# Twelve normalized tiles turned by TensorE instead of through DRAM, row units that leave PSUM early, and later transfers in SyncE's order

## The chip, the cores and the metric

The kernel runs on one core of a Trainium2 chip. The core has TensorE (PE) for matrix products, VectorE (DVE), ScalarE (ACT) and GpSimd (POOL) for elementwise work, and SyncE (SP), which here issues nearly all DMA transfers; 16 DMA engines carry them out. Each engine works through its own instructions in order and waits on semaphores for the others. The metric is the device time of one execution in microseconds. Before the change its median is 3538.62 us over 3 runs (3537.95 to 3542.44).

## The reference

One transformer block with conditional normalization, in float32, over x of 8 x 1024 x 512, with 16 heads of width 32 and a hidden width of 2048:

```python
mod = silu(condition) @ Wada + bada
sh_a, sc_a, gt_a, sh_m, sc_m, gt_m = split(mod, 6, axis=1)
xm = layernorm(x, g1, be1) * (1 + sc_a) + sh_a
x = x + gt_a * (softmax(mask(q k^T) * 32 ** -0.5) v @ Wproj + bproj)   # q, k, v = xm @ Wqkv
xm = layernorm(x, g2, be2) * (1 + sc_m) + sh_m
x = x + gt_m * (gelu(xm @ W1 + b1) @ W2 + b2)
```

The mask is causal: a query sees the keys up to its own place.

## The kernel before, in words

**Blocks.** The 8 x 1024 tokens are cut into NB = 16 blocks of 512 tokens, numbered n; an even block is the first half of a sequence, an odd one the second. Every block goes through the first norm (tiles `hat_a`, `xm_a`), the products k, q and v, attention, the output product (`project_out`), the second norm (`hat_m`, `xm_m`), `up` (four steps with a gelu) and `down` (four parts).

**Two streams.** Attention is one stream; the linear work of neighbouring blocks is the other and is woven into it. The linear work follows `plan`: beside block w, roughly the rest of `down` for block w - 2, v, the output product and second norm of block w - 1, k and q for block w + 1, then `up` for w - 1. The order of all instructions is written when the kernel is built. A planner keeps a clock for each engine (`now`), the time at which each result is believed ready (`written`) and the time at which a buffer is free (`left`); `note`, `note_pe`, `note_act` and `note_dma` advance them. `work` advances that thread of linear work which waits least by this reckoning; `step_aside` puts linear work ahead of an attention step whose inputs are not believed ready. `jobs`, `row_jobs` and `act_jobs` are queues of elementwise work, and `sooner` and `either` choose between two engines by the same clocks. On the chip the order is fixed, and an instruction that comes to its place too early holds up everything behind it on its engine.

**Weights.** The linear products use one level of Strassen's scheme on 256 x 256 pieces. The pieces come through a ring of 8 slots (`fetch`, L347 to L363); SyncE issues each load when TensorE has freed the slot. All transfers stand in SyncE's one queue: weights, x, residuals, turned tiles and attention images.

**Turning a normalized tile.** The norm is computed with tokens on partitions, and the products need features there. Tiles named in `by_pe` (a0, a1, m0, m1, m14, m15) are turned by TensorE in `modulated`: for each of four feature chunks four 128 x 128 transposes against the identity go into one of the three PSUM banks (L778), then one VectorE or ScalarE instruction (L782, L788) applies scale and shift on the way to SBUF. All other tiles go through `turn`: VectorE turns 32 x 32 blocks (L714) into the space of `xm`, SyncE writes 1 MB to DRAM as `held` (L723), four transfers of 256 KB bring it back in turned order (L728), and four instructions apply scale and shift. For such tiles x is loaded in another order of rows too (L412 instead of L410).

**Attention by rows.** Odd blocks, and block 0, compute scores twice: once for the row maxima (`scores_at_once`), once transposed for the weights (`weights_T`, exponentials at L1734). Even blocks from 2 on, seven of them, are row blocks (`attend_rows`). A row unit (`rows_unit`) puts the scores of four heads, queries by keys, into `st`, a set of four PSUM banks that is there once for all score work. In the kernel before, VectorE adds the mask in place (L2028), takes the maxima (L2032) and scales them (L2034), and ScalarE reads `st` for the exponentials with their sums and writes `rows_p` in SBUF (L2040). VectorE turns 32 x 32 blocks (`turned`, L2053), SyncE writes an image to DRAM (`scatter`, L2068), and `gather` reads pages of it back in turned order (L2143) for the products with v (L2155). `inverses` sends the reciprocals of the sums the same way (L2097, L2105). There are three SBUF slots for units and pages, and at most two units may stand between scores and image at a time. Each row block has ten units: four of one part with 512 keys, four of two parts with 384 and 128 keys, and two of two parts with 256 keys each. That makes 70 units and 112 parts.

**What sets the order around the change.** The planner's ready times decide where SyncE's transfers stand; a transfer is written into the order when its input is believed ready:

```python
note("DVE", 620, [("hat", key, t)], done)
nc.sync.dma_start(held, small_blocks)
note_dma(2600, [("blocks", key)], [("held", key)])
yield [("held", key)], []
```

Of the kernel before, what the change touches and what calls it, by code (L numbers as in the profile page):

```python
# [9 lines left out]
F32 = mybir.dt.float32  # L10
BF16 = mybir.dt.bfloat16
AF = mybir.ActivationFunctionType
# [10 lines left out]
def kernel(  # L23
# [370 lines left out]
        r0 += n  # L394
    O_G1, O_BE1, O_G2, O_BE2, O_BPROJ, O_B2, O_B1, O_BADA = at

    by_pe = {"a0", "a1", "m0", "m1", f"m{NB - 2}", f"m{NB - 1}"}
    Q = P // NTT

    def hat_tile(key):  # L400
# [305 lines left out]
    def turn(key, rows, xm):  # L706

        small_blocks = xm.rearrange("p c n -> p (c n)")
        by_tile = small_blocks.rearrange("p (m h t i) -> p h m t i", m=NTT, h=NC, t=NTT)
        written["blocks", key] = NEVER  # L710

        def turn_tile(t):
            into = by_tile[:, :, :, t, :]
            nc.vector.transpose(into, rows[:, t, :].rearrange("p (h m i) -> p h m i", m=NTT, i=Q))  # L714
            done = [("blocks", key)] if t == NTT - 1 else []
            note("DVE", 620, [("hat", key, t)], done)

        for t in range(NTT):
            add_job(lambda t=t: turn_tile(t), [("hat", key, t)], key[0] == "m")
        yield [("blocks", key)], []  # L720
        held = kept.tile([P, NTT * D], F32, tag=f"held_{turns[0] % 2}", name=f"held_{key}")
        turns[0] += 1
        nc.sync.dma_start(held, small_blocks)  # L723
        note_dma(2600, [("blocks", key)], [("held", key)])
        yield [("held", key)], []
        for m in range(NTT):
            some = held[:, ts(m, D)].rearrange("(a i) d -> i a d", i=Q)
            nc.sync.dma_start(rows[ts(m, Q), :, :], some)  # L728
            note_dma(1250, [("held", key)], [("turned", key)])
        yield [("turned", key)], []  # L730
# [1267 lines left out]
    def rows_unit(n, g, parts):  # L1998

        until(lambda: n in projected)  # L2000
        until(lambda: free_p and len(raws) < 2)
        slot = take_slot()
        raws.append(slot)
        reads = [("qT", n), ("kT", n)]
        step_aside(reads, ["st", ("p", slot)])
        name = f"{n}_{g}_{parts[0][0]}"
        sc = ps_st.tile([P, HPG, TB], F32, tag="st", name=f"rows_sc_{name}")
        raw = pp.tile([P, HPG * TB], F32, tag=f"p{slot}", name=f"rows_p_{name}")
        mx, minus = (
            small.tile([P, 2, HPG], F32, tag=f"rows_{kind}", name=f"rows_{kind}_{name}")  # L2010
            for kind in ("max", "minus")
        )
        for gg in {part[4]: None for part in parts}:
            if (n, gg) not in totals_of:
                totals_of[n, gg] = small.tile(
                    [P, HPG, NTT], F32, tag=f"rows_sum_{gg}", name=f"rows_sum_{n}_{gg}", bufs=1
                )
        for qt, kh, c0, w, gg in parts:
            for j in range(HPG):
                r = slice(j * hd, (j + 1) * hd)  # L2020
                nc.tensor.matmul(  # L2021
                    sc[:, j, c0 : c0 + w], qTs[n][r, gg, ts(qt, P)], kTs[n][r, gg, :w],
                    start=True, stop=True, skip_group_check=True,
                )
# [3 lines left out]
        nc.vector.tensor_tensor(place, place, shape_of.to_broadcast(place.shape), ALU.add)  # L2028
        note("DVE", 165 + 4.16 * span, ["st"])
        n_parts = len(parts)  # L2030
        for i, (qt, kh, c0, w, gg) in enumerate(parts):
            nc.vector.tensor_reduce(mx[:, i, :], sc[:, :, c0 : c0 + w], axis=AX.X, op=ALU.max)  # L2032
            note("DVE", 170 + 4.14 * w, ["st"], [("mxr", slot)])
        nc.vector.tensor_scalar(minus[:, :n_parts], mx[:, :n_parts], -scale, None, ALU.mult)  # L2034
        note("DVE", 120, [], [("mxr", slot)], port=True)
        places, at = [], 0
        for i, (qt, kh, c0, w, gg) in enumerate(parts):
            tile_of = raw[:, at : at + HPG * w].rearrange("p (b k j x) -> p j k b x", b=NTT, j=HPG, x=hd)
            for j in range(HPG):
                nc.scalar.activation(  # L2040
                    tile_of[:, j], sc[:, j, c0 : c0 + w].rearrange("p (k b x) -> p k b x", b=NTT, x=hd),
                    AF.Exp, bias=minus[:, i, j : j + 1], scale=scale, accum_out=totals_of[n, gg][:, j, qt : qt + 1],
                )
                note_act(480 + 0.82 * w, "exp", ["st", ("mxr", slot)], [("p", slot)])
            places.append((qt, w, gg, at))
            at += HPG * w
            in_sums[n, gg] += 1
            if in_sums[n, gg] == NTT:
                written["sums", n, gg] = written["p", slot]
                start(inverses(n, gg))  # L2050

        def turned():
            nc.vector.transpose(raw, raw)  # L2053
            note("DVE", 2320, [("p", slot)], [("p", slot)])
            start(scatter())

        def scatter():
            yield [("p", slot)], []
            for qt, w, gg, at in places:
                count = w // P  # L2060
                if (n, gg) not in images:
                    images[n, gg] = [
                        kept.tile([P, 2, NTT, size, P], F32, tag=f"image_{gg}_{size}", name=f"image_{n}_{gg}_{size}")
                        for size in (2, 4)
                    ]
                for a in range(NTT):
                    into = images[n, gg][qt // 2][:, qt % 2, a, :count, :]
                    nc.sync.dma_start(  # L2068
                        into.rearrange("(b k) s e -> k b (s e)", k=hd),
                        raw[ts(a, hd), at : at + HPG * w].rearrange("k (b f) -> k b f", b=NTT),  # L2070
                    )
# [12 lines left out]
    def inverses(n, g):  # L2084

# [202 lines left out]
```

## Time and profile before

| what | us |
|---|---|
| median of 3 runs | 3538.62 |
| the profiled execution | 3545.22 |
| its span, first to last instruction | 3543.5 |
| TensorE busy | 3377.7 |
| VectorE busy | 2339.5 |
| GpSimd busy | 1762.9 |
| ScalarE busy | 1248.8 |

Busy time is the time in which an engine worked on instructions. Matmuls overlap in TensorE, so one that is shown with 379 ns follows the one before it much sooner, and a group of four on different columns of the array runs at the same time. The mean granted clock of TensorE over the execution is 0.985 of its full rate. A row of the waits names who waited, for whom, the total, the number and the longest. A row of the groups gives line, engine, operation, tiles, shapes and count, then busy time and mean ns of one, then the engine's idle time before them and what ended it. The chain of work is followed back from the last instruction, at each step to what released it.

### The profile page before, as it was taken

To read this page: it belongs to the slowest core of one execution; us is meant where nothing else is said; L and a number is where in the kernel's file an instruction comes from. 1 tells how busy PE (TensorE), PEld (TensorE's weight loads), DVE (VectorE), ACT (ScalarE), POOL (GpSimd) and SP (SyncE) were. 2 spreads that over 40 slices of the span, in tenths; PEclk is the share of its full clock that TensorE was granted. 3 is DMA by queue.
4 is the path that set the end of the run, shared out by engine and by line. 5 is a ranking of instruction groups with operands and counts; after the bars stand their busy time and mean duration, and the time that the engine had idled before them with its cause. 6 is when DMAs were issued, how large, how long until landed. Compare 5 with 4: busy or idle time off the path is not lost.

```text
span 3543.5 us, 118795 instructions
## 1 busy us (share of the span) xinstructions
PE 3377.7 (95%) x52861; PEld 1705.4 (48%) x52861; DVE 2339.5 (66%) x2562; ACT 1248.8 (35%) x1970; POOL 1762.9 (50%) x1710
## 2 busy tenths in 40 slices
PE   8999889999899998999999999999999999899999
PEld 4444445444454444544454454544555445454455
DVE  5766577657577575775767757676677667566563
ACT  2334333343233532335223353333523334232521
POOL 3667713756037650477405674066731667208640
PEclk9999999999999999999999999999999999999999
DMA  6843487537875378753886538865498555973344
GB/s 198 263 148 112 150 235 214 155 109 213 245 209 155 102 226 239 209 153 103 247 233 189 153 109 264 253 185 142 127 284 236 147 142 154 284 221 111 92 135 138
DMA packets 502579, 645.42 MB, mean 182 GB/s; under 512 B 40365, under 2 KB 334061, under 8 KB 498485
## 3 DMA queue, kind: packets, MB, share of 16 engines
q1 hardware_dynamic: 501952, 637.80, 60.8%
q8 instruction: 416, 6.82, 0.8%
q14 instruction: 95, 0.77, 0.1%
q10 hardware_dynamic: 116, 0.03, 0.0%
HBM read 506.31 MB, written 129.27 MB: 179 GB/s over the span
## 4 chain that ended last, share of the span: by engine, by line
PE 37%; DMA 6%; POOL 4%; DVE 3%; issue 1%; SPq 1%; ACT 1%; DVEq 0%; POOLq 0%; ACTq 0%
PE bank L217 27%; PE sc L1613 3%; POOL pT L1856 3%; PE po L1762 2%; PE st L1721 2%; DMA held_m<-xm_m 1%; DMA turned<-image 1%; PE rows_sc L2021 1%; PE st L1709 1%; PE po L2155 1%; DVE mx L1628 1%; DMA w<-in_L_cond_Wproj_dram 1%; DMA hat_m<-held_m 1%; PE bank L1783 0%; DMA w<-in_L_cond_W_dram 0%
## 5 line engine op out<-in xcount | busy, mean ns | idle before, releaser
L1856 POOL TENSOR_TENSOR pT<-pT,pT 128x512 f32<-128x512 f32 (+3 forms) x918 | 981.9, 1104 | 250.5 <-ACT pT L1734 197.2
L217 PE MATMUL bank<-w,hT 128*32 128x256 f32 x14336 | 822.4, 380 | 0.9 <-ACT y_d L204 0.9
L1734 ACT ACTIVATE pT<-st 128x2048 f32<-128x2048 f32 x218 | 409.5, 1879 | 762.1 <-PE st L1721 573.9
L217 PEld LDWEIGHTS bank<-w,hT 128*32 128x32 f32 x14336 | 457.0, 110 | 372.7 <-issue 87.5
L1628 DVE TENSOR_REDUCE mx<-sc 128x4 f32<-128x2048 f32 (+3 forms) x271 | 499.4, 1859 | 183.0 <-PE sc L1613 179.7
L217 PE MATMUL bank<-xm_m,w 128*32 128x256 f32 x8192 | 506.6, 384 | 28.8 <-DMA w<-in_L_cond_W_dram 19.7
L2040 ACT ACTIVATE rows_p<-rows_sc,rows_minus 128x256 f32<-128x256 f32 (+3 forms) x448 | 229.6, 534 | 448.0 <-DVE rows_minus L2034 246.4
L217 PE MATMUL bank<-t_m,w 128*32 128x256 f32 x6144 | 382.9, 380 | 1.1 <-DVE hT L208 0.9
L217 PEld LDWEIGHTS bank<-xm_m,w 128*32 128x32 f32 x8192 | 257.8, 111 | 245.5 <-issue 66.4
L217 PEld LDWEIGHTS bank<-t_m,w 128*32 128x32 f32 x6144 | 190.7, 110 | 179.8 <-issue 58.3
L217 PE MATMUL bank<-xm_a,w 128*32 128x256 f32 x3968 | 252.1, 392 | 26.0 <-DVE xm_a L782 16.3
L217 PE MATMUL bank<-w,qT 128*32 128x512 f32 x2048 | 242.0, 610 | 16.3 <-DMA w<-in_L_cond_Wproj_dram 16.2
L1613 PE MATMUL sc<-kT,qT 32*128 32x512 f32 (+3 forms) x2168 | 250.6, 546 | 6.9 <-DVE mx L1628 3.5
L1762 PE MATMUL po<-pT,v 128*32 128x512 f32 (+3 forms) x2176 | 232.0, 515 | 4.5 <-POOL pT L1739 4.4
L1721 PE MATMUL st<-qT,kT 32*128 32x512 f32 (+3 forms) x2176 | 228.5, 508 | 0.0
L208 DVE TENSOR_TENSOR hT<-bank,u_u 128x512 f32<-128x512 f32 x181 | 121.4, 683 | 113.0 <-PE bank L217 110.6
L217 PEld LDWEIGHTS bank<-xm_a,w 128*32 128x32 f32 x3968 | 131.7, 113 | 131.3 <-issue 29.2
L217 PE MATMUL bank<-t_a,w 128*32 128x256 f32 x2944 | 184.4, 383 | 2.6 <-DVE qT L208 2.1
L2053 DVE STREAM_TRANSPOSE rows_p<-rows_p 128x2048 f32<-128x2048 f32 x70 | 160.9, 2298 | 36.2 <-ACT rows_p L2040 35.5
L1625 DVE TENSOR_TENSOR sc<-sc,mask 128x1024 f32<-128x1024 f32 (+1 forms) x89 | 90.5, 1017 | 124.4 <-PE sc L1613 91.9
L1129 ACT ACTIVATE hT<-hT,cols 128x512 f32<-128x512 f32 x256 | 164.4, 711 | 22.8 <-DVE hT L208 21.6
L655 POOL TENSOR_SCALAR rstd_a<-mv_a 128x4 f32<-128x4 f32 x14 | 3.2, 231 | 333.6 <-DVE mv_a L634 333.1
(268 smaller groups left out, 4152.9 us busy)
## 6 DMA issues: line engine op xcount, KB each, us to landing
w<-in_L_cond_W_dram SPq DMA_DIRECT2D x384, 256.0 KB
w<-kept_up_S SPq DMA_DIRECT2D x256, 256.0 KB
w<-kept_down_S SPq DMA_DIRECT2D x256, 256.0 KB
w<-kept_qkv_S SPq DMA_DIRECT2D x180, 256.0 KB
w<-in_L_cond_Wqkv_dram SPq DMA_DIRECT2D x147, 256.0 KB
image<-rows_p SPq DMA_DIRECT2D x112, 256.0 KB
turned<-image SPq DMA_DIRECT2D x28, 1024.0 KB
turned<-image SPq DMA_DIRECT2D x56, 512.0 KB
```

The source lines that it names most:

```text
L208: nc.vector.tensor_tensor(out, src, other, op)
L217: nc.tensor.matmul(ps[r, :], columns, rhs, start=start, stop=stop, skip_group_check=True)
L1129: nc.scalar.activation(hT[:, i, :], hT[:, i, :], AF.Gelu, bias=cols[:, O_B1 + f : O_B1 + f + 1])
L1613: nc.tensor.matmul(sc[:, j, c0 : c0 + w], qTs[n][r, gg, ts(qt, P)], keys_of(n, kh)[r, gg, :w], start=True, stop=True, skip_group_check=True,)
L1625: nc.vector.tensor_tensor(place, place, shape_of.to_broadcast(place.shape), ALU.add)
L1628: nc.vector.tensor_reduce(maxima[n, gg][:, kh, qt, :], sc[:, :, c0 : c0 + w], axis=AX.X, op=ALU.max)
L1721: nc.tensor.matmul(st[:, j, c0 : c0 + w], kT[r, gg, ts(k % NTT, P)], qT[r, gg, TB - w :], start=False, stop=True, skip_group_check=True,)
L1734: nc.scalar.activation(pT[:, :, :used], st[:, :, :used], AF.Exp, scale=scale)
L1762: nc.tensor.matmul(po[r, TB - w :], v[:, k % NTT, g * P + j * hd : g * P + (j + 1) * hd], pT[:, j, c0 : c0 + w], start=(k == 0), stop=last ...
L1856: nc.gpsimd.tensor_tensor(into, into, pT[:, j, c0 : c0 + w], ALU.add)
L2040: nc.scalar.activation(tile_of[:, j], sc[:, j, c0 : c0 + w].rearrange("p (k b x) -> p k b x", b=NTT, x=hd), AF.Exp, bias=minus[:, i, j : j ...
L2053: nc.vector.transpose(raw, raw)
```

## The change

Four things change.

1. `by_pe` gets a5, a7, ... a15 and m3, m5, ... m13. These twelve tiles are the ones that are turned while an even block is attended by rows.
2. `rows_unit` empties `st` at once: VectorE adds the mask to the last 128 keys of each part while it writes them to `rows_p`, and ScalarE copies the other keys, 128 at a time. The maxima are a job of its own (`largest`), the exponentials a thread of its own (`exponentials`), and both work on `rows_p` in SBUF, in place. The small tiles for maxima get two buffers by name.
3. Four ready times are set later: blocks of a turned tile by 1200 ns, `held` by 2500, a turned row unit by 2000, the rows of reciprocals by 2500.
4. Nothing else is edited, but as the order is planned, instructions move on all engines. Counted in the order: TensorE has 192 more transposes, VectorE 48 fewer of its block transposes, SyncE 60 fewer transfers, ScalarE 168 more copies; the table loads of ScalarE are 6 more, and some elementwise work changes its engine.

```diff
-    by_pe = {"a0", "a1", "m0", "m1", f"m{NB - 2}", f"m{NB - 1}"}
+    by_pe = (({"a0", "a1", "m0", "m1", f"m{NB - 2}", f"m{NB - 1}"}) | {f"a{n}" for n in range(5, NB, 2)}) | {f"m{n}" for n in range(3, NB - 1, 2)}
...
             note("DVE", 620, [("hat", key, t)], done)
+            for one in done:
+                written[one] += 1200
...
         note_dma(2600, [("blocks", key)], [("held", key)])
+        written["held", key] += 2500
...
-        span, place = diagonals(parts, sc)
-        shape_of = mask.unsqueeze(1).unsqueeze(1)
-        nc.vector.tensor_tensor(place, place, shape_of.to_broadcast(place.shape), ALU.add)
-        note("DVE", 165 + 4.16 * span, ["st"])
-        n_parts = len(parts)
-        for i, (qt, kh, c0, w, gg) in enumerate(parts):
-            nc.vector.tensor_reduce(mx[:, i, :], sc[:, :, c0 : c0 + w], axis=AX.X, op=ALU.max)
-            note("DVE", 170 + 4.14 * w, ["st"], [("mxr", slot)])
-        nc.vector.tensor_scalar(minus[:, :n_parts], mx[:, :n_parts], -scale, None, ALU.mult)
         places, at = [], 0
-        for i, (qt, kh, c0, w, gg) in enumerate(parts):
+        shape_of = mask.rearrange("p (b x) -> p b x", x=hd).unsqueeze(1)
+        for qt, kh, c0, w, gg in parts:
             tile_of = raw[:, at : at + HPG * w].rearrange("p (b k j x) -> p j k b x", b=NTT, j=HPG, x=hd)
-            for j in range(HPG):
-                nc.scalar.activation(
-                    tile_of[:, j], sc[:, j, c0 : c0 + w].rearrange("p (k b x) -> p k b x", b=NTT, x=hd),
-                    AF.Exp, bias=minus[:, i, j : j + 1], scale=scale, accum_out=totals_of[n, gg][:, j, qt : qt + 1],
+            into = tile_of[:, :, w // P - 1]
+            some = sc[:, :, c0 + w - P : c0 + w].rearrange("p j (b x) -> p j b x", x=hd)
+            nc.vector.tensor_tensor(into, some, shape_of.to_broadcast(into.shape), ALU.add)
+            for k in range(w // P - 1):
+                nc.scalar.copy(
+                    tile_of[:, :, k],
+                    sc[:, :, c0 + k * P : c0 + (k + 1) * P].rearrange("p j (b x) -> p j b x", x=hd),
                 )
...
+        def largest():
+            for i, (qt, w, gg, at) in enumerate(places):
+                some = raw[:, at : at + HPG * w].rearrange("p (a j x) -> p j a x", j=HPG, x=hd)
+                nc.vector.tensor_reduce(mx[:, i, :], some, axis=AX.XY, op=ALU.max)
+            ...
+            start(exponentials())
+
+        def exponentials():
+            yield [("mxr", slot)], []
+            for i, (qt, w, gg, at) in enumerate(places):
+                some = raw[:, at : at + HPG * w].rearrange("p (a j x) -> p j a x", j=HPG, x=hd)
+                for j in range(HPG):
+                    nc.scalar.activation(
+                        some[:, j], some[:, j], AF.Exp, bias=minus[:, i, j : j + 1], scale=scale,
+                        accum_out=totals_of[n, gg][:, j, qt : qt + 1],
+                    )
+            ...
+            row_jobs.append((turned, [("p", slot)]))
 
         def turned():
             nc.vector.transpose(raw, raw)
             note("DVE", 2320, [("p", slot)], [("p", slot)])
+            written["p", slot] += 2000
             start(scatter())
...
-        row_jobs.append((turned, [("p", slot)]))
+        row_jobs.append((largest, [("raw", slot)]))
...
         note_dma(150, ["rec"], [("rows back", n, g)])
+        written["rows back", n, g] += 2500
```

More of the change, by code (lines that the diff above doesn't have):

```diff
@@ L2009, in rows_unit @@
         mx, minus = (
-            small.tile([P, 2, HPG], F32, tag=f"rows_{kind}", name=f"rows_{kind}_{name}")
+            small.tile([P, 2, HPG], F32, tag=f"rows_{kind}", name=f"rows_{kind}_{name}", bufs=2)
             for kind in ("max", "minus")
@@ L2043, in rows_unit @@
                 )
-                note_act(480 + 0.82 * w, "exp", ["st", ("mxr", slot)], [("p", slot)])
+                note_act(585, None, ["st"], [("raw", slot)])
             places.append((qt, w, gg, at))
             at += HPG * w
[L2047 to L2050, printed above, removed]
+        def largest():
+            for i, (qt, w, gg, at) in enumerate(places):
+                some = raw[:, at : at + HPG * w].rearrange("p (a j x) -> p j a x", j=HPG, x=hd)
+                nc.vector.tensor_reduce(mx[:, i, :], some, axis=AX.XY, op=ALU.max)
+                note("DVE", 170 + 4.14 * w, [("raw", slot)], [("mxr", slot)])
+            n_parts = len(places)
+            nc.vector.tensor_scalar(minus[:, :n_parts], mx[:, :n_parts], -scale, None, ALU.mult)
+            note("DVE", 120, [], [("mxr", slot)], port=True)
+            start(exponentials())
@@ new lines, in exponentials @@
+        def exponentials():
[7 more added lines that the diff above has]
+                    )
+                    note_act(480 + 0.82 * w, "exp", [("mxr", slot)], [("p", slot)])
+                in_sums[n, gg] += 1
+                if in_sums[n, gg] == NTT:
+                    written["sums", n, gg] = written["p", slot]
+                    start(inverses(n, gg))
+            row_jobs.append((turned, [("p", slot)]))
```

2 lines of the change are left out of this document (1 added, 1 removed).

## The prediction

> **What bounds the kernel now.** I read the page's head first, then a table of stages, then TensorE's waits, then the chain of work through one of those waits.
>
> ```profile
> span 3543.5 us, 118795 instructions
> PE 3377.7 (95%) x52861; PEld 1705.4 (48%) x52861; DVE 2339.5 (66%) x2562; ACT 1248.8 (35%) x1970; POOL 1762.9 (50%) x1710
> ```
>
> TensorE is busy for 3377.7 of 3543.5 us. No other engine passes 66%, so the end is TensorE's own work plus the 165.8 us in which it stands. The table of stages says where it stands. Each row gives a stretch, then the busy time of TensorE, its weight loads, VectorE, ScalarE and GpSimd, the granted clock, the DMA share and GB/s. The first row is a stretch without row blocks; the other seven are the early parts of the row blocks 2, 4, 6, ... 14.
>
> ```profile
> 200.00:300.00 100.00, 100.00 (x1496) 47.54 (x1496) 63.38 (x72) 49.21 (x49) 65.16 (x69) 1.00 0.44 126
> 400.00:500.00 100.00, 78.41 (x1039) 36.09 (x1032) 65.23 (x75) 34.00 (x101) 33.78 (x35) 0.88 0.66 198
> 850.00:950.00 100.00, 84.37 (x1312) 44.33 (x1304) 62.04 (x83) 24.04 (x71) 24.26 (x21) 0.95 0.92 272
> 1300.00:1400.00 100.00, 84.46 (x1300) 42.93 (x1300) 58.21 (x78) 22.16 (x62) 13.06 (x13) 0.93 0.86 258
> 1750.00:1850.00 100.00, 90.91 (x1412) 48.55 (x1416) 57.87 (x75) 22.28 (x48) 11.62 (x11) 0.93 0.85 246
> 2150.00:2250.00 100.00, 89.58 (x1456) 49.22 (x1452) 60.62 (x82) 21.43 (x61) 22.20 (x20) 0.97 0.92 281
> 2600.00:2700.00 100.00, 89.51 (x1416) 47.25 (x1412) 60.52 (x78) 24.10 (x60) 10.30 (x10) 0.95 0.89 258
> 3025.00:3125.00 100.00, 87.84 (x1396) 46.87 (x1392) 56.53 (x75) 23.52 (x59) 15.19 (x14) 0.97 0.84 247
> ```
>
> The seven stretches idle for 100 minus their second figure: 21.6, 15.6, 15.5, 9.1, 10.4, 10.5 and 12.2, together 94.9 us. In the six later ones the DMA engines are 84% to 92% busy and the granted clock is 0.93 to 0.97; in the first row the DMA is at 44%, the clock at 1.00 and TensorE never idle. What TensorE waits for (total, times, longest):
>
> ```profile
> PE bank L217 <- DMA w<-in_L_cond_W_dram: 19.7, 3, 7.5
> PE po L2155 <- DMA turned<-image: 17.1, 19, 3.2
> PE bank L217 <- DVE xm_a L782: 16.3, 2, 8.6
> PE bank L217 <- DMA w<-in_L_cond_Wproj_dram: 16.2, 11, 4.5
> PE rows_sc L2021 <- ACT rows_p L2040: 12.5, 4, 7.9
> PE bank L217 <- ACT xm_m L788: 2.8, 2, 2.1
> PE sc L1613 <- ACT rows_p L2040: 2.1, 2, 1.4
> ```
>
> These seven rows are 86.7 us. The chain at block 8 (start, length, what), and the turn of block 5 in order of time, show what stands behind them:
>
> ```profile
> 1784.94 10.20 DMA held_m<-xm_m
> ...
> 1796.50 7.43 DMA hat_m<-held_m
> ...
> 1804.47 5.01 DMA w<-in_L_cond_W_dram
> ```
>
> ```profile
> 876.27 0.33 SPq L723 DMA_DIRECT2D held_a<-xm_a  x1
> ...
> 897.04 1.01 DVE L782 TENSOR_SCALAR xm_a<-hat_a,gaina,shifta 128x512 f32<-128x512 f32 x2 [4.11 <-DMA hat_a<-held_a]
> ...
> 897.64 0.65 PE L217 MATMUL bank<-xm_a,w 128*32 128x256 f32 x4 [8.65 <-DVE xm_a L782]
> ```
>
> A turn through DRAM takes 876.27 to 897.04, 20.8 us from write to use, and in block 8 1784.94 to 1803.93, 19.0 us. The weight of the next step comes after it in SyncE's queue (issued 1804.47) and TensorE stands again.
>
> **The change, part by part.**
>
> *The turn.* Twelve tiles (a5 to a15 and m3 to m13, odd) leave the DRAM route. What goes and what one costs:
>
> ```profile
> held_m<-xm_m SPq DMA_DIRECT2D x12, 1024.0 KB
> hat_m<-held_m SPq DMA_DIRECT2D x48, 256.0 KB
> L714 DVE STREAM_TRANSPOSE xm_m<-hat_m 128x512 f32<-128x512 f32 x48 | 30.2, 679 | 0.0
> L728 SPq DMA_DIRECT2D hat_m<-held_m x48: 303/424/1413, 687.4 to 3085.0; - x48
> ```
>
> Per tile one write and four reads go, 2 MB, and five issues at about 0.42 us. At 272 GB/s (stretch 850 to 950) 2.1 MB are 7.7 us of all DMA engines, so two tiles free about 15 us of some 92 busy in each of six stages. VectorE loses 48 transposes of 0.679, 32.6 us, with none idle before them. The loads of x keep their count and bytes. Added are 192 transposes on TensorE, four to a bank:
>
> ```profile
> 211.39 0.66 PE L778 MATMUL bank<-ident,hat_m 128*128 128x128 f32 x4
> 211.97 0.42 PE L217 MATMUL bank<-t_a,w 128*32 128x256 f32 x4
> L778 PE MATMUL bank<-ident,hat_m x64: 272/273/477, 211.4 to 3440.6; 128*128 128x128 f32 x64
> ```
>
> From a group's start to the next matmul are 0.58 us, change of form included; 48 groups make 27.8 us. The bounds are 0 (all in time in which TensorE stands anyway) and 192 x 0.272 = 52 us (nothing overlaps). I take 27.8: it is the cost in a stretch without idle time. TensorE may also wait for a bank to be emptied, as these rows show for the tiles that it turns already:
>
> ```profile
> PE bank L778 <- DVE xm_m L782: 1.3, 1, 1.3
> PE bank L778 <- ACT xm_a L788: 1.2, 1, 1.2
> ```
>
> That is 0 for m0 and about 1.2 for m1 and a1: bounds 0 and 14 for twelve tiles; I take half of the upper per tile, 6 (nearest to the mean of the tiles shown). Scale and shift remain four per tile, now from a bank on ScalarE or VectorE; these have room (24% and 62% in the stretch 850 to 950).
>
> Against that the two waits for xm_a (16.3) and those for xm_m (2.8) go, since write, landing, read and landing go. The weight waits: W stands behind the turn in the queue, so I take 15 of 19.7 (bounds 19.7 and 0). Wproj comes ahead of the block's own m turn and is helped only by the lower DMA load: 5 of 16.2 (same bounds). Pages of turned rows compete with the same traffic: 8 of 17.1 (bounds 17.1 gained and 17.1 lost, as the margins below hold pages longer).
>
> *The row units.* Today the bank set "st" of a unit is released after mask, maxima and exponentials. Afterwards mask and copies release it, and maxima and exponentials work in SBUF.
>
> ```profile
> L2028 DVE TENSOR_TENSOR rows_sc<-rows_sc,mask 128x1024 f32<-128x1024 f32 x42 | 51.3, 1221 | 27.6 <-PE rows_sc L2021 27.3
> L2028 DVE TENSOR_TENSOR rows_sc<-rows_sc,mask 128x512 f32<-128x512 f32 x28 | 19.3, 691 | 10.6 <-PE rows_sc L2021 10.5
> L2032 DVE TENSOR_REDUCE rows_max<-rows_sc 128x4 f32<-128x2048 f32 x28 | 64.2, 2292 | 1.0
> L2040 ACT ACTIVATE rows_p<-rows_sc,rows_minus 128x512 f32<-128x512 f32 x112 | 75.5, 686 | 163.6 <-DVE rows_minus L2034 48.2 <-DMA turned<-image 34.6 <-issue 27.5
> L197 ACT COPY hT<-bank 128x512 f32<-128x512 f32 x41 | 23.9, 582 | 96.4 <-PE bank L217 96.3
> ```
>
> For the widest unit the release falls from 0.69 + 2.29 + 4 x 0.69 = 5.7 us to three copies of 0.58 beside a mask of 0.69, 1.7 us. ScalarE gets 168 copies x 0.582 = 98 us, 14 per row block; the masks become 112 x 0.691 = 77.4 instead of 70.6. Both lie beside TensorE while ScalarE is under 25% busy there; without that cover the 14 us per block delay every later unit. Maxima and exponentials keep count and size; from SBUF I cost them at nothing (bounds a tenth either way, 23 us over the run, off the path). The waits of rows_sc and sc for rows_p are 14.6: I take 12 (bounds 14.6 gained; 14 lost, one block's copies).
>
> *The margins.* The planner now believes that blocks are ready 1.2 us later, held and rows back 2.5 and turned units 2.0, so it writes these transfers and their readers later. SyncE stands with everything behind it when one comes too early:
>
> ```profile
> SPq L360 <- PE bank L217: 949.2, 478, 20.1
> SPq L723 <- DVE xm_a L714: 31.4, 6, 16.5
> SPq L2068 <- DVE rows_p L2053: 29.9, 13, 7.1
> SPq L723 <- DVE xm_m L714: 16.2, 3, 7.0
> SPq L728 <- DMA held_m<-xm_m: 14.8, 9, 3.4
> ```
>
> The last four are 92.3 us, against 949.2 in which the queue waits for TensorE to free weight slots. Behind them stand the weights. I gave their worth to the weight and page waits above. The price is that a slot of a unit is held some 2 us longer and pages start later; the work of the other steps hides it while there is some, else it is the page bound above.
>
> *The clock.* The stretches with gaps have 0.93 to 0.97. If all 527 us busy in the six ran at 1.00 instead of a mean of 0.95, 26 us would go; I take 6, as most of the low share lies in the gaps themselves (bounds 15 and 0).
>
> *Sum.* 27.8 + 6 - 16.3 - 2.8 - 15 - 5 - 8 - 12 - 6 = -31.3 us. The profiled execution took 3545.2 (span 3543.5 and 1.7 around it), so 3513.9. It lies 6.6 over the median of 3538.6, which gives **3507**.
>
> **A rule that speaks against it.** In the full stretch 200 to 300 TensorE turns tile m0 between other work, and the granted clock stays at 1.00. If the clock fell to half while TensorE turns a tile, the 27.8 would double and the sum be -3.5, 3535; the 0.88 to 0.97 of the other stretches shows that it does fall when TensorE does too little. The Trainium skill, "TensorE: Matmul & The Clock Gate", Part 4, says that transposes do not count as activity for the clock gate in the way matmuls do; by that rule this case would come, and the row of 200 to 300 does not agree with it.
>
> **The rivals.**
> - *Queue order, not volume, is the limit* (slower). The weight waits remain since SyncE's queue is held by free slots (949.2), not by turns, and pages come later and double their 17.1: 27.8 + 6 - 19.1 - 12 + 17.1 = +19.8, **3558**. It decides when W, Wproj and pages together give back less than 3 us. For it: that figure. Against: W is issued 0.5 us after the turn's landing.
> - *ScalarE holds "st"* (slower). Copies stand behind the previous unit's exponentials, 8 x 0.69 = 5.5 us; if this hits 10 of 70 units and the 12 gained go: -31.3 + 12 + 55 = +36, 3574. Against: 24% busy.
> - *All of it goes*: 86.7 of waits and 15 of clock against 33.8: -68, **3471**.
> - *The waits only move*: weight and page waits stay as they are, clock too: 33.8 - 31.1 = +3, 3541.
> - *The clock falls in the turns*: 3535, as worked out above.
>
> **How the numbers follow.** Forecast 0.50, all goes 0.18, queue order 0.15, ScalarE 0.06, waits move 0.06, clock 0.05. Within 0.2% (7 us, about what a measurement of this kernel tells from no change) are the last two, 0.11; faster 0.68, slower 0.21. The range runs from 3471 to the queue case, 3558; only the ScalarE case and the tails of its neighbours lie outside. The forecast's own range is 3485 to 3528.
>
> **What would show it.** Transposes: 288 instead of 96, a group near 0.6 us to the next matmul. Idle in the six later stretches down from 73 to about 35 us, no wait of TensorE on xm_a, W waits under 5. rows_sc waits on ScalarE under 3. DMA 25 MB less in all. If page waits rise above 17 us or W stays near 20, the queue case holds; if rows_sc waits on copies, the ScalarE case.

## The result, and the profile after

The changed kernel takes 3581.47 us (median of 4 runs, 3575.97 to 3588.03), the kernel before 3539.32 us (4 runs, 3537.95 to 3542.44) beside it. The ratio is 1.0119, with a 95% interval from 1.0099 to 1.0138: slower by 1.2%. The forecast was 3507, the range ended at 3558.

The head of the profile after:

```profile
span 3582.2 us, 119193 instructions
PE 3396.4 (95%) x53053; PEld 1715.4 (48%) x53053; DVE 2344.8 (65%) x2575; ACT 1367.2 (38%) x2161; POOL 1725.9 (48%) x1671
```

The span grew by 38.7 us: TensorE is busy 18.7 us longer, with 192 more transposes in it, and stands 185.8 us instead of 165.8. The stretches that the prediction looked at, taken anew for the changed kernel (columns as before). The six later ones begin 31 to 35 us after the first row unit of their block; in the kernel before they began 32 to 68 us after it:

```profile
200.00:300.00 100.00, 99.24 (x1436) 45.49 (x1432) 66.08 (x74) 42.05 (x40) 66.83 (x67) 1.00 0.43 125
420.00:520.00 100.00, 87.11 (x1244) 41.35 (x1240) 80.81 (x93) 51.01 (x142) 15.44 (x18) 0.95 0.82 236
850.00:950.00 100.00, 94.84 (x1500) 51.23 (x1492) 63.33 (x80) 34.87 (x102) 21.20 (x19) 0.98 0.79 240
1280.00:1380.00 100.00, 94.22 (x1532) 50.02 (x1528) 58.83 (x74) 27.36 (x72) 25.60 (x22) 1.00 0.82 249
1710.00:1810.00 100.00, 94.53 (x1476) 52.14 (x1480) 62.56 (x75) 27.07 (x70) 30.39 (x24) 0.95 0.80 238
2145.00:2245.00 100.00, 90.02 (x1396) 47.36 (x1388) 63.31 (x76) 31.45 (x87) 35.70 (x26) 0.97 0.81 242
2585.00:2685.00 100.00, 93.00 (x1496) 50.75 (x1492) 65.63 (x80) 31.46 (x87) 35.67 (x26) 1.00 0.86 262
3025.00:3125.00 100.00, 92.44 (x1456) 49.37 (x1445) 64.77 (x78) 31.46 (x87) 35.69 (x26) 0.98 0.82 255
```

The six later stretches stand 5.2 + 5.8 + 5.5 + 10.0 + 7.0 + 7.6 = 41 us instead of 73; 35 were forecast. With the offsets of before they stand 44 us. In the place looked at, the forecast nearly came true. The loss is elsewhere. A table of stages that counts whole stages, the seven row blocks first (from the first row unit to the first transposed scores of the next block), then, from 73 us on, all that lies between them, gives these sums of length and of TensorE's busy time. The kernel before:

```profile
sum 1447.20, PE 1336.41; mean PE 190.92
sum 2022.80, PE 1981.11; mean PE 247.64
```

The kernel after:

```profile
sum 1352.90, PE 1247.70; mean PE 178.24
sum 2156.40, PE 2090.45; mean PE 261.31
```

The row stages became 94 us shorter and the others 134 us longer. Idle time is 110.8 and 41.7 us before, 105.2 and 66.0 after: what went in the early part of the row stages came back in their later part and in the stages between. TensorE's waits after:

```profile
PE po L2177 <- DMA turned<-image: 31.6, 21, 4.5
PE st L1712 <- DVE mx L1631: 16.3, 13, 3.9
PE sc L1616 <- DVE mx L1631: 14.9, 12, 2.4
PE bank L1786 <- ACT hT L204: 13.4, 3, 4.5
PE bank L217 <- ACT p_k L197: 10.4, 5, 2.4
...
PE sc L1616 <- ACT rows_p L2038: 6.3, 7, 1.0
PE sc L1616 <- DVE rows_p L2035: 6.1, 7, 0.9
PE bank L217 <- DVE u_v L208: 5.6, 3, 2.3
PE bank L217 <- DMA w<-in_L_cond_Wproj_dram: 5.4, 1, 5.4
PE bank L1669 <- DVE mcols L1653: 5.3, 5, 1.4
...
PE rows_sc L2024 <- DVE rows_p L2035: 4.6, 1, 4.6
PE bank L1669 <- POOL mcols L1653: 4.0, 3, 1.6
```

W (the waits for `in_L_cond_W_dram`) is gone from this list, of `xm_a` 0.2 us is left, and Wproj fell from 16.2 to 5.4. In their place stand waits for VectorE and ScalarE. The group of the new copies on the page, and one place in order of time, show how such a wait comes about:

```profile
L2038 ACT COPY rows_p<-rows_sc 128x512 f32<-128x512 f32 x168 | 89.9, 589 | 370.5 <-DVE rows_p L2035 287.7
```

```profile
2554.14 5.35 DVE L167 TENSOR_TENSOR xr<-xr,row_gbm 128x512 f32<-128x512 f32 x4
...
2559.41 3.42 DVE L1229 TENSOR_TENSOR hT<-hT 128x1024 f32<-128x1024 f32 x2
...
2562.76 0.68 DVE L2035 TENSOR_TENSOR rows_p<-rows_sc,mask 128x512 f32<-128x512 f32 x1
2563.53 0.59 ACT L2038 COPY rows_p<-rows_sc 128x512 f32<-128x512 f32 x1 [11.66 <-DVE rows_p L2035]
...
2565.35 0.59 ACT L204 COPY hT<-bank 128x512 f32<-128x512 f32 x1
...
2566.09 1.52 PE L1786 MATMUL bank<-pT,ones 128*32 128x512 f32 x8 [4.48 <-ACT hT L204]
```

A copy (L2038) does not run beside the mask (L2035) of its unit: it starts 0.77 us after the start of the mask, which takes 0.68, since it waits on a semaphore for the mask. Both read `rows_sc`, in the same four banks of `st`, and both write `rows_p`; which of the two the semaphore guards is taken up in the last section. The mask stands behind 8.8 us of other work on VectorE, so ScalarE stands for 11.66 us with a copy at its head; behind that copy is the one that empties a bank (L204), and TensorE stands for the bank. The planner doesn't know: it books the copy with `["st"]` as all it waits for.

### The profile page after: what moved, and what is told of

Same layout as the page of the kernel before. It is cut to its first block, busy times and chain, and to the rows that moved or that the text cites. A ratio compares the mean times of both kernels' runs of the same rounds, so it can differ in the third digit from the quotient of the medians.

```text
span 3582.2 us, 119193 instructions
## 1 busy us (share of the span) xinstructions
PE 3396.4 (95%) x53053; PEld 1715.4 (48%) x53053; DVE 2344.8 (65%) x2575; ACT 1367.2 (38%) x2161; POOL 1725.9 (48%) x1671
## 4 chain that ended last, share of the span: by engine, by line
PE 68%; DVE 13%; DMA 8%; POOL 4%; ACT 3%; issue 2%; SPq 2%; ACTq 0%; DVEq 0%; POOLq 0%
PE bank L217 47%; PE sc L1616 5%; PE po L1765 5%; PE st L1724 5%; DMA turned<-image 4%; DVE mx L1631 3%; POOL pT L1859 2%; PE st L1712 2%; PE po L2177 1%; DMA image<-rows_p 1%; DVE rows_max L2049 1%; ACT rows_p L2038 1%; PE rows_sc L2024 1%; PE bank L1786 1%; DVE rows_p L2035 1%
## 5 line engine op out<-in xcount | busy, mean ns | idle before, releaser
L1859 POOL TENSOR_TENSOR pT<-pT,pT 128x512 f32<-128x512 f32 (+3 forms) x918 | 996.1, 1119 | 304.5 <-ACT pT L1737 135.6
L217 PE MATMUL bank<-w,hT 128*32 128x256 f32 x14336 | 823.1, 382 | 9.1 <-DVE y_d L208 5.1
L217 PEld LDWEIGHTS bank<-w,hT 128*32 128x32 f32 x14336 | 455.7, 110 | 379.2 <-issue 86.2
L217 PE MATMUL bank<-xm_m,w 128*32 128x256 f32 x8192 | 504.7, 381 | 4.7 <-DVE p_u L194 2.4
L217 PE MATMUL bank<-t_m,w 128*32 128x256 f32 x6144 | 381.4, 380 | 3.3 <-DVE hT L208 1.5
L217 PEld LDWEIGHTS bank<-xm_m,w 128*32 128x32 f32 x8192 | 252.4, 110 | 236.4 <-issue 62.7
L217 PEld LDWEIGHTS bank<-t_m,w 128*32 128x32 f32 x6144 | 191.8, 110 | 169.2 <-issue 40.2
L2061 ACT ACTIVATE rows_p<-rows_p,rows_minus 128x256 f32<-128x256 f32 (+3 forms) x448 | 245.3, 551 | 60.0 <-DVE rows_minus L2052 59.8
L217 PE MATMUL bank<-xm_a,w 128*32 128x256 f32 x3968 | 245.1, 383 | 10.4 <-ACT p_k L197 10.4
L217 PE MATMUL bank<-w,qT 128*32 128x512 f32 x2048 | 241.9, 613 | 8.3 <-DMA w<-in_L_cond_Wproj_dram 5.4
L2038 ACT COPY rows_p<-rows_sc 128x512 f32<-128x512 f32 x168 | 89.9, 589 | 370.5 <-DVE rows_p L2035 287.7
L1650 POOL CAST mcols<-mx 128x16 bf16<-128x16 f32 x31 | 13.0, 419 | 418.4 <-DVE mx L1645 402.1
L217 PE MATMUL bank<-t_a,w 128*32 128x256 f32 x2944 | 184.5, 381 | 0.8 <-DVE qT L208 0.8
L217 PEld LDWEIGHTS bank<-xm_a,w 128*32 128x32 f32 x3968 | 128.9, 111 | 116.6 <-issue 29.2
```

The costliest lines, as they stand in the source:

```text
L217: nc.tensor.matmul(ps[r, :], columns, rhs, start=start, stop=stop, skip_group_check=True)
L1859: nc.gpsimd.tensor_tensor(into, into, pT[:, j, c0 : c0 + w], ALU.add)
L2038: nc.scalar.copy(tile_of[:, :, k], sc[:, :, c0 + k * P : c0 + (k + 1) * P].rearrange("p j (b x) -> p j b x", x=hd),)
L2061: nc.scalar.activation(some[:, j], some[:, j], AF.Exp, bias=minus[:, i, j : j + 1], scale=scale, accum_out=totals_of[n, gg][:, j, qt : qt ...
```

## The experiments

Theories put up first. A: the row units cost, because ScalarE's copies stand behind VectorE's mask. B: a turn on TensorE isn't worth its 21 us of work, the stalls only move. C: the order before is fitted to its constants, and any other order costs. Formed on the way, and tested in the later runs: A2, it isn't the copies' wait that costs but that the planner is not told of it; D, deferring maxima and exponentials makes pages late; E, the row stages hold too little linear work. All times are in us; idle is the span less TensorE's busy time in the profiled execution.

| run | edit against the kernel before | median | ratio to before, 95% | idle |
|---|---|---|---|---|
| e1 | turn | 3562.52 | 1.0046 [1.0024, 1.0068] | 158.5 |
| e2 | units | 3588.56 | 1.0126 [1.0103, 1.0149] | 197.8 |
| e3 | later times ("margins") | 3559.77 | 1.0047 [1.0030, 1.0063] | 184.8 |
| e4 | turn, margins | 3571.41 | 1.0075 [1.0049, 1.0101] | 171.5 |
| e7 | turn, m tiles only | 3556.88 | 1.0026 [1.0010, 1.0041] | 180.2 |
| e8 | turn, a tiles only | 3558.12 | 1.0037 [1.0016, 1.0058] | 151.2 |
| e9 | units, copies ahead of the mask | 3586.02 | 1.0108 [1.0091, 1.0125] | 212.3 |
| e11 | nothing but a constant, 110 ns | 3559.88 | 1.0040 [1.0026, 1.0054] | 184.3 |
| e14_sync_90 | the same constant, 90 ns | 3568.61 | 1.0068 [1.0050, 1.0086] | 194.3 |
| e14_sync_120 | the same, 120 ns | 3567.87 | 1.0067 [1.0052, 1.0082] | 191.0 |
| e12 | units, nothing deferred | 3667.21 | 1.0339 [1.0321, 1.0358] | 273.8 |
| e10 | units, booking put right ("told") | 3550.12 | 1.0016 [1.0006, 1.0027] | 170.3 |
| e23 | units, constant 110 | 3621.33 | 1.0216 [1.0196, 1.0237] | 235.8 |
| e24 | units told, constant 110 | 3575.14 | 1.0075 [1.0048, 1.0101] | 192.7 |
| e16 | the whole change, told | 3548.23 | 1.0007 [0.9996, 1.0019] | 148.8 |
| e17 | turn, units told | 3543.81 | 0.9991 [0.9976, 1.0006] | 139.5 |
| e21 | turn of a tiles, units told | 3541.80 | 0.9989 [0.9975, 1.0003] | 156.5 |
| e25 | as e17, pages expected later | 3532.39 | 0.9970 [0.9956, 0.9984] | 134.4 |

### The parts, one at a time

e1, the turn alone:

```diff
-    by_pe = {"a0", "a1", "m0", "m1", f"m{NB - 2}", f"m{NB - 1}"}
+    by_pe = (({"a0", ...}) | {f"a{n}" for n in range(5, NB, 2)}) | {f"m{n}" for n in range(3, NB - 1, 2)}
```

> The kernel before with the longer by_pe alone: TensorE turns the twelve tiles, row units and ready times as before. Theory A (the row units are what costs: ScalarE's copies stand behind VectorE's mask and hold up ScalarE's queue): turning alone gains, since the waits for xm_a (16.3 us) and W (19.7 us) go for about 21 to 28 us of transposes; 3515 to 3530. Theory B (the turn is not worth its work: TensorE pays 21 us and the stalls only move): 3550 to 3560. Theory C (any change of the order costs, since the order before is fitted to the constants): 3550 to 3570 here, and the same in the other two single edits.

e2, the row units alone (the diff of `rows_unit`, nothing else):

> The kernel before with the new row units alone, no further turns, ready times as before. Theory A: block 2 gains up to 20 us, as its waits on st go, but the later blocks lose 8 to 12 us each; 3555 to 3590. Theory B: 3515 to 3530, as only the gain of block 2 is left. Theory C: 3550 to 3570.

e3, the four later times alone, and e4, turn and later times:

```diff
+                written[one] += 1200
+        written["held", key] += 2500
+            written["p", slot] += 2000
+        written["rows back", n, g] += 2500
```

> The kernel before with the four later ready times alone. Theory A: 3530 to 3545, little either way. Theory B: the same. Theory C: 3550 to 3570. If the margins are what makes pages late, the waits of the products with v for pages (17.1 us before, 31.6 after the change) rise here to about 30 us.

> The change without its row units: longer by_pe and later ready times. Theory A: faster than before, 3505 to 3525, the wait of the sum of weights for a bank that ScalarE empties (13.4 us after the change) is gone. Theory B: 3550 to 3560. Theory C: 3560 to 3580.

Each part alone is slower, and the units by most, 1.26% where the whole change is 1.19%. So the first half of theory A, by which e1 and e4 would be faster, does not hold. In e3 the page waits are 25.8 us (about 30 were expected if the later times make pages late), W is 0.6 and Wproj 37.4. TensorE's waits in the run of the turn:

```profile
PE rows_sc L2021 <- ACT rows_p L2040: 27.5, 11, 7.9
PE bank L778 <- DVE y_d L208: 22.6, 6, 5.0
...
PE po L2155 <- DMA turned<-image: 12.7, 11, 2.8
```

W and `xm_a` are gone here too. But the third group of transposes waits for a bank whose content (`y_d`) VectorE is to take out, and VectorE first works through a row unit's mask and maxima:

```profile
828.74 2.29 DVE L2032 TENSOR_REDUCE rows_max<-rows_sc 128x4 f32<-128x2048 f32 x1
...
832.53 0.68 DVE L208 TENSOR_TENSOR y_d<-bank,p_d 128x512 f32<-128x512 f32 x1
...
833.27 1.12 PE L778 MATMUL bank<-ident,hat_a 128*128 128x128 f32 x4 [4.33 <-DVE y_d L208]
```

The wait of the row units for `st` is 27.5 here, 12.5 before. With the units the maxima stand elsewhere: in the changed kernel the `y_d` wait ahead of transposes is 2.2 us.

e7 and e8 split the turn:

```diff
+    by_pe = {... as before ...} | {f"m{n}" for n in range(3, NB - 1, 2)}     # e7
+    by_pe = {... as before ...} | {f"a{n}" for n in range(5, NB, 2)}         # e8
```

> The kernel before with only m3 to m13 turned by TensorE. If the price of turning is the bank that an a tile must wait for (22.6 us of TensorE's waits on y_d, all at hat_a in the run with all turns), these waits are absent here and W stays gone: 10 us of transposes against 19.7 of W, so 3530 to 3540. If turning never pays since the stalls only move: 3550 or more.

> The kernel before with only a5 to a15 turned by TensorE. If the bank is the price: about 20 us of waits on y_d against 16.3 of xm_a, and 10 us of transposes, W stays at 15 to 20: 3555 to 3570. If it is not: no wait on y_d above 5 us.

The halves cost 0.26% and 0.37%, together somewhat more than the whole turn. The ranges of single times are wide (3545.7 to 3574.4 and 3541.8 to 3574.5) and the two profiled executions lie at opposite ends, so their idle times say little. The wait on `y_d` is 16.6 us in e8 and absent in e7, as expected; but e7 is slower than the kernel before as well, where 3530 to 3540 was expected, so that bank is not the whole price of turning. W is 1.5 in e8, though the m tiles still go through DRAM there, and 0.6 in e3, where all twelve tiles do. That W stands because of the turn is therefore not shown.

### What an order is worth

e11 and its two fellows change no work, only the planner's constant for a semaphore. Some instructions change places, and a few elementwise ones their engine (in e11 VectorE has 2559 instead of 2562, ScalarE 1973 instead of 1970, GpSimd 1706 instead of 1710):

```diff
-    SYNC, PIPE, SWITCH, TABLE = 100, 250, 150, 1283
+    SYNC, PIPE, SWITCH, TABLE = 110, 250, 150, 1283
```

> The kernel before with the planner's constant for one semaphore at 110 instead of 100 ns: no instruction is added or removed, only the order moves. If the order before is fitted to its constants (theory C), 3550 to 3565. If not, within 7 us of the kernel before.

> The kernel before with the planner's constant for a semaphore 90 ns instead of 100: no instruction is added or removed, some stand elsewhere. Theory C (the order before is fitted; every other order costs): slower by 0.2 to 0.6%, 3552 to 3567, with the added idle time in a few single waits, in the stretch up to 425 us too. If the effect of order is without direction: between 3525 and 3565, and faster as likely as slower.

> The same with 120 ns. Theory C: slower by 0.2 to 0.8%, 3552 to 3575. Without direction: 3525 to 3565.

All three are slower, by 0.40 to 0.68%. With 110 ns most of the added idle time lies ahead of the first row unit. The sums for the stretch from 73 to 425 us, before and with 110 ns:

```profile
sum 352.00, PE 338.16; mean PE 338.16
```

```profile
sum 352.00, PE 324.54; mean PE 324.54
```

That is 13.8 us of idle time against 27.5, 13.7 of the 18.5 us that e11 stands longer. With 90 and 120 ns it is only 7.4 of 28.5 and 4.8 of 25.2. With the later times of e3 the stretch stands 20.8, in the changed kernel 20.1 from 72.9 to 418.4. So the 0.46 and 0.47% of e1 and e3 are no more than a mere change of order costs: three orders of three speak for theory C. That the order before was fitted is argued, not shown, and not every other order costs: e16, e17 and e25 below, with other work in them, are no slower than the kernel before.

### What makes the units cost

e9 lets the copies go first:

```diff
+            for k in range(w // P - 1):
+                nc.scalar.copy(...)
             nc.vector.tensor_tensor(into, some, shape_of.to_broadcast(into.shape), ALU.add)
-            for k in range(w // P - 1):
-                nc.scalar.copy(...)
```

> The new row units alone, with ScalarE's copies written ahead of VectorE's mask in each part, so that ScalarE need not wait for VectorE (287.7 us of ScalarE's waits after the change). If ScalarE's queue behind the mask is what costs: that wait is gone, and the time falls from 3589 to 3555 or lower. If the longer way of a unit (pages late, work shifted) costs: it stays within 10 us of 3589.

The time stays. The wait has changed sides:

```profile
DVE rows_p L2038 <- ACT rows_p L2031: 142.2, 53, 9.8
...
ACT rows_p L2031 <- DVE rows_p L2038: 23.8, 14, 6.2
```

Theory A as it stood falls: it isn't ScalarE's standing that costs. But in both versions one of the two engines stands where the planner believes it at work. That is A2.

e12 issues maxima and exponentials in the unit itself:

```diff
-            start(exponentials())
+            exponentials()
...
-        row_jobs.append((largest, [("raw", slot)]))
+        largest()
```

> Row units alone, but maxima and exponentials are issued in the unit itself and not as a job that waits for its turn, as before; mask and copies still release 'st' first. Theory D, the deferral makes pages and slots late: page waits (po on turned) fall from 29 to under 20 us and the time to 3555 to 3568. Theory E (the row stages are left with less linear work; here even less, 77 to 153 us per stage by the order against 93 to 156): no gain, 3580 to 3600.

It is the slowest of all, and the page waits rise (here `po` is at L2171):

```profile
PE po L2171 <- DMA turned<-image: 60.5, 25, 8.5
```

The deferral is a gain in this order, and theory D is refuted. E isn't excluded by this run.

e10 moves nothing by hand; it tells the planner that a copy comes after the mask of its unit. As the planner keeps a write behind the reads that it knows (`left`), the same key also books the next mask of a unit behind the copy:

```diff
-                note_act(585, None, ["st"], [("raw", slot)])
+                note_act(585, None, ["st", ("raw", slot)], [("raw", slot)])
```

> Row units alone (no turns, no margins), but the planner is told what the hardware does: a ScalarE copy of a unit's tile is booked as starting after VectorE's mask of the same tile. Theory A2, the units cost because the planner believes 'st' free too early (ScalarE copies waited 260 us for the mask in the run of the units alone): with the true times in the plan at least half of the 43 us go, 3555 to 3568, and TensorE's waits of sc and rows_sc for rows_p fall below 8 us. Theory E, the units cost because the row stages hold some 20 us less linear work per block, which the following stages have no need of: no change, 3580 to 3595. Theory C (any order but the fitted one costs): 3555 to 3595, tells nothing alone.

The ratio falls from 1.0126 to 1.0016. The copies wait no less, 260.4 us in e2 and 287.6 here. What changed is who stands behind them. From the waits of e2, then of e10:

```profile
ACT rows_p L2035 <- DVE rows_p L2032: 260.4, 61, 13.1
...
PE sc L1613 <- DVE rows_p L2032: 11.2, 11, 2.3
...
PE sc L1613 <- DVE mx L1628: 11.0, 9, 2.4
...
PE sc L1613 <- ACT pT L1734: 10.7, 6, 4.3
```

```profile
ACT rows_p L2035 <- DVE rows_p L2032: 287.6, 67, 20.1
...
PE sc L1613 <- DVE rows_p L2032: 2.7, 1, 2.7
...
PE sc L1613 <- DVE mx L1628: 2.6, 2, 2.4
...
PE sc L1613 <- ACT pT L1734: 2.2, 2, 1.4
```

32.9 us of waits for `sc` became 7.5. In all, the span of the profiled execution falls by 38.5 us: 27.5 less idle, and 11.0 less busy time for the same 52861 matmuls (3385.0 to 3374.0, at a mean granted clock of 0.979 and 0.983). Theory E, which expected no change, falls here. As an order alone can be worth 24 us, the pair was repeated under the constant of 110 ns, untold (e23) and told (e24):

> Units alone as in the change, planned with 110 ns for a semaphore. Theory A2: the cost of the units stays whatever the constant, 3580 to 3605. Theory C: anything between 3550 and 3600, not systematically above its told twin.

> The twin of the run before it with the booking of the copies put right. Theory A2: 20 to 45 us under its twin, 3548 to 3572. Theory C: within 12 us of its twin or above it.

3621 against 3575: 46 us between the twins, 38 in the first pair (by the ratios, 1.1% of 3545 is 39). A2 holds in both, though both times of this pair lie above what was expected (3580 to 3605 and 3548 to 3572).

### The whole, told

e16 is the changed kernel with that one booking put right, e17 the same without the later times:

> The changed kernel whole, with the one booking put right: a copy is planned as starting after the mask of its tile. Theory A2, the planner's wrong belief about the copies is what made the changed kernel slower: 3538 to 3560, TensorE's waits of sc and rows_sc for rows_p from 17 to under 8 us. Theory C, the told units were a lucky order: 3565 to 3590, as the sum of turn (+16), margins (+17) and units has no such term.

> Turns and units with the right booking, the four later times left out. Theory A2: turn +16 and told units +6 give 3550 to 3568. Theory B, the turn's 21 us of added work have no stall left to fill once the units are told: the upper half of that, 3560 to 3568; if the turn fills stalls beside told units: 3535 to 3550. Theory C: 3565 to 3590.

e16 stands at 1.0007, so the booking accounts for the 1.2% by which the changed kernel was slower. It is the third pair that differs in this key alone, and in all three the idle time falls, by 27.5, 43.1 and 37.0 us (busy time by 11.0, 3.8 and -1.6). With the stages cut as above, the row stages of e16 idle 61.8 us instead of 105.2 and the rest 73.8 instead of 66.0, so the gain lies in the row stages. Whether the true time or any later time for the copies would do, the pairs don't tell. Its copies still wait 239.4 us for the mask, but the waits of `sc` and `rows_sc` for `rows_p` and that of L1786 for ScalarE are no longer in the list. What is late next are the pages:

```profile
ACT rows_p L2038 <- DVE rows_p L2035: 239.4, 60, 16.0
...
PE po L2177 <- DMA turned<-image: 52.6, 24, 6.5
```

e17 has 34.5 of these, and 0.9991. The later times make the page waits longer in each pair that differs in them alone: 17.1 to 25.8 (e3), 12.7 to 25.1 (e1 and e4), 34.5 to 52.6. The first pair is hardly clear of an order's effect, as they are 24.0 with 120 ns. Beside told units alone (1.0016) the turn seems to give back more than its work: 31 us less idle (170.3 to 139.5) for 22 us more busy time (3374.0 to 3395.6). The difference of the two ratios, 0.25%, is less than a mere order can make, so theory B (no gain) is doubted here and not refuted; alone (e1) the turn bore it out.

e21 keeps the a half of the turn, e25 all of e17 with another constant, which sets pages 1.5 us later and images and inverses 0.75:

```diff
-    LATE = 3000
+    LATE = 4500
```

> Told units with the turn on TensorE for the six tiles a5 to a15 only; the m tiles take the DRAM route. Told units alone stood at 1.0016, with all twelve turns at 0.9991. If the turns pay back: between the two, 3538 to 3552, idle between 135 and 166 us, no wait for xm_a. If the gain with twelve was the order's luck: over 3555.

> Told units and twelve turns, and the planner expects a page 4.5 us after its booked landing instead of 3.0. If the page waits (34.5 us) come from a booking that is too early: page waits under 20 us and 3520 to 3538, faster than both kernels. If TensorE has nothing else to do there, the waits turn into others: 3538 to 3560; a changed order alone moved the time by 0.4 to 0.7%.

e21 is no different from e17 in time, so that half the turns give half the effect was not shown. Its idle time, 156.5, lies where it was expected; 2.2 us of waits for `xm_a` are left. In e25 the page waits fall, by less than hoped:

```profile
PE po L2172 <- DMA turned<-image: 25.8, 11, 5.9
```

With 0.9970 [0.9956, 0.9984] it is faster than both kernels. How much of its last 0.2% is the page booking and how much a better order stays open; one run of a changed order moved by more than that.

## Why the prediction was wrong, by its own steps

| term | forecast | changed kernel | e16, the booking put right |
|---|---|---|---|
| transposes | +27.8 | TensorE's whole busy time +18.7 | +20.3 |
| waits for a bank ahead of them | +6 | 5.7 to 11.1: +5.4 | +5.1 |
| `xm_a`, `xm_m` | -19.1 | gone, but for 0.2 | gone |
| W | -15 | 19.7, gone | -19.1 |
| Wproj | -5 | 16.2 to 5.4: -10.8 | -8.6 |
| pages | -8 | 17.1 to 31.6: +14.5 | 52.6: +35.5 |
| units' waits (`sc`, `rows_sc` for `rows_p`) | -12 | 14.6 to 17.0: +2.4 | gone: -14.6 |
| clock | -6 | within the busy time | within the busy time |
| `st` and `sc` for VectorE's maxima `mx` | none | 12.4 to 31.2: +18.8 | -4.5 |
| L1786 for `hT`; L217 for `p_k` and `u_v`; `mcols` | none | 7.0 to 38.7: +31.7 | -0.7 |

The column of the changed kernel adds up to +41.9, its span grew by 38.7; that of e16 to -5.7, its span grew by 3.3. Other rows are left out. The 11.1 is the sum of the idle times before the transposes:

```profile
L781 PE MATMUL bank<-ident,hat_m 128*128 128x128 f32 x160 | 26.8, 297 | 6.6 <-ACT hat_m L701 3.4 <-ACT hat_m L674 1.7 <-DVE xm_m L785 1.4
L781 PE MATMUL bank<-ident,hat_a 128*128 128x128 f32 x128 | 20.4, 303 | 4.5 <-ACT xm_a L791 2.3 <-DVE y_d L208 2.2
```

*The turn* came out near its size in the whole change: the waits for `xm_a` went and 25.1 MB less were moved, 25 forecast. Its bank waits held there; alone they were 22.6 for `y_d` only, over the bound of 14, which came from tiles that are turned where no row unit runs, and the turn alone cost 0.46%. The reason given for W, that it stands behind the turn in the queue, is not shown (0.6 in e3 and 1.5 in e8, with m tiles still going through DRAM); that its term came true may be luck.

*The row units* are the step that failed: "three copies of 0.58 beside a mask of 0.69, 1.7 us" and "Both lie beside TensorE while ScalarE is under 25% busy there". The copies don't run beside the mask: they waited 287.7 us for it, which neither the sum nor the planner had booked. The term of -12 came out at +2.4. The wait by itself is not the price: in e16 the copies still wait 239.4 us, the term is there (-14.6), and the ratio is 1.0007 instead of 1.0119. The price is what the plan sets behind a copy that it believes at work, evictions and scores for which TensorE then stands. The busy share of ScalarE, 38%, doesn't show that. The rival "ScalarE holds `st`" came out within 8 us of the time (3574), but it had the copies behind the exponentials of the unit before; they stood behind VectorE. It got 0.06, on the busy share.

*The margins*, priced at the page bound: alone 0.47%, in the told kernel 1.0007 with and 0.9991 without them. Neither stands clear of what a mere change of order costs, though pages wait 52.6 with and 34.5 without.

*Pages* are the second step that failed, and by this sum the reason why even e16 isn't faster. In the changed kernel they stayed within the bounds with the wrong sign. In e16 they are at +35.5, outside the bound of 17.1, while each other term that the prediction sized on a row lies within 8 us of its forecast. The told units alone wait 37.4 us for pages (e10), turn and told units 34.5 (e17), and the later times add 18.1. Why the units' pages come later stays open: with nothing deferred (e12) they wait longer still. The queue-order rival's 17.1 more is near the measured 14.5, but its other half, weights that stay, is refuted in the changed kernel.

*The clock.* The mean granted clock is 0.985 before and 0.986 after, and the stretches 1280 to 1380 and 2585 to 2685, which hold newly turned tiles, are at 1.00. So the rival in which the clock falls is refuted. The term of -6 left no mark on the mean either, though the clock in the six later stretches rose, from between 0.93 and 0.97 to between 0.95 and 1.00. The rule of the Trainium skill, "TensorE: Matmul & The Clock Gate", Part 4, that transposes don't count as activity for the clock gate in the way matmuls do, finds no support here: these stretches hold 16 and 32 transposes among some 1500 matmuls and show no lower clock. So few among so many matmuls do not refute the rule either.

*The method.* I summed waits that would go and bounded those that I could name. The planner writes the whole order anew, and 50.5 of the 91.5 us on the losing side stand in rows that the sum had no term for. A chance of 0.68 for faster left that out.

## What to carry to other kernels

In a kernel whose order is planned, a new instruction must be booked with every wait that the built program will hold, also those between two engines that work on one tile or one set of banks; one missing key cost 38 to 46 us here, and was put right in one line. Ask of an added instruction what stands ahead of its inputs and what is queued behind it, not how busy its engine is. Before a part of 0.5% is believed good or bad, run a reorder that changes no work: here it cost 0.40 to 0.68%.

## What was not expected of the hardware

The mask and the copies of a unit, on two engines and on different columns, worked in turns: in the place shown the copy started 0.77 us after the start of a mask of 0.68, and the next mask of the unit waited for the copy (47.3 us in 42 such waits over the execution). The waits are a semaphore's, so the program's and not the engines' own. In the view of the copies' line (count, then least, median and longest in ns):

```profile
L2038 ACTq EVENT_SEMAPHORE  x164: 17/38/10937, 444.7 to 3173.1; - x164
```

Sharing an SBUF tile does not always do this. In the changed kernel both engines write parts of one `hat_a` tile at the same time:

```profile
2549.22 2.97 DVE L669 TENSOR_SCALAR hat_a<-hat_a,rstd_a,offset_a 128x512 f32<-128x512 f32 x2
...
2551.06 0.80 ACT L674 ACTIVATE hat_a<-hat_a,offset_a,rstd_a 128x512 f32<-128x512 f32 x1
```

The mask of a unit's second part and the copy of its first write separate stretches of `rows_p`; what they share beside that tile are the four banks of `st` that both read. That speaks for the banks as the reason, but no run separates the two, and two tiles for `rows_p` were not tried. Moving maxima and exponentials off PSUM changed their length little: the widest takes 2268 ns from SBUF against 2292, an exponential of 512 columns 713 against 686.
